# A decoder block in one kernel: three product-key units prepared beside the attention to the context, and three expert tiles put in a conditional block

## The chip, the core and the metric

The kernel runs on one core of one Trainium2 chip. The time is the device time of one execution in microseconds (us), from the first to the last instruction of the program and the little that lies around it. TensorE is called PE, its weight load PEld, VectorE DVE, ScalarE ACT, GpSimd POOL, SyncE SP.

## What is computed

All numbers are 32-bit floats. `x` has 16 sequences of 256 tokens with 256 features, `ctx` has 16 contexts of 120 rows. Cut to what matters:

```python
x = x + self_attention(layernorm(x))               # 16 heads, rotary, causal
x = x + attention_to(ctx)(layernorm(x))            # 16 heads, biases
x = x + product_keys(layernorm(x))                 # below
x = x + band_attention(layernorm(x))               # 16 heads, +0.1 near the diagonal
x = x + context_flow(layernorm(x), ctx)            # bi-directional attention flow
x = x + experts(layernorm(x))                      # below

def product_keys(x):                               # per token, 8 heads
    q1, q2 = halves(x @ Wq + bq)                   # 2 x 32 per head
    v1, i1 = top_k(q1 @ K1.T, 10)                  # 64 keys each
    v2, i2 = top_k(q2 @ K2.T, 10)
    vals, best = top_k(v1[:, None] + v2[None, :], 10)
    h = gelu(x @ W_down[chosen].T) * softmax(vals)
    return h @ W_up[chosen]

def experts(x):                                    # 8 experts, 2 per token
    w = softmax(x @ Wr + br), kept for the two largest, normalised
    return sum(w[e] * (relu(x @ W1[e] + b1[e]) @ W2[e] + b2[e]) for e in two)
```

## The kernel before, in words

All of `x` stays in SBUF as 16 tiles `xt[b]` of 128 partitions x 2 x 256, one for a sequence (a *batch* here). The work comes in five stages, one behind the other; each opens its own pools of SBUF and PSUM, so that its first tiles and its first loads wait until the stage before has let go of the memory.

**Both first attentions** are one pipeline (`run`, L149). It goes through 32 sequences of work (16 batches of the self-attention, then 16 of the attention to the context), six stages deep: `prepare`, `ready`, `maxima`, `weigh`, `values`, `finish`. In a round `v` the stage `i` works on batch `v - i`. `maxima` and `weigh` are the *joint* stages: their score matmuls (L246) are woven pair by pair, and behind each pair DVE takes the row maxima (L274) and ACT the exponentials (L315). The others are generators; `others_go(k)` moves them on by `k` steps, in turn, between two pairs (`gap` of them), and what is left goes at the end of the round. The order on PE is that order, by hand (`manual_schedule`). On the other engines a scheduler orders the instructions. `fresh` (L113) makes the layernorm statistics for four batches at a time (L119, L120, L122, L123), `normalized` (L103) writes `xn`, `transposed` (L126) gives `xnT`. Both tags have two buffers here. The score tiles `sa` and `sb` have one PSUM buffer each. Every tile of the small projections shares the PSUM tag `t1` with two buffers.

**The product keys** (L533 to L811) work on 32 *units* of 128 tokens. Four parts follow each other, one round of the loop apart: `front` (L557: normalise, transpose, project with `wq`, L137, and multiply by the keys, L581), `lists` (L585: the 16 best of 64 keys for 8 heads x 2 halves, all on DVE, in 8 steps), `choice` (L608: the best sums, on DVE, POOL and ACT, ending in `slots`), `places` and `spread` (L707, L725: one-hot tiles on DVE, L714, and POOL, L721, multiplied on PE, L733, into a `gate`), and `dense` (L744: all 4096 hidden values, L137, gelu, gate, and the second product, L758). In round `v`, `front` is at unit `v+1`, `lists` at `v`, `choice` at `v-1`, `spread` at `v-2`, `dense` at `v-3`. The loop starts at `v = -1`, so `dense` has nothing to do in its first four rounds. PE and DVE follow the written order. Ahead of the loop `layernorm_stats` (L95) makes the statistics of all 32 units (L98 to L102) and `shift` (L767). The stage loads `wq`, `keys12`, `w_dn` (2 x 2 MB) and `w_up` (4 MB) on SP when its pool opens (L538 to L543). The zeroing of the buffer `rows` (L763) is written in this stage too, but it needs nothing, and the scheduler starts it at the head of the kernel.

**The band attention** is the same pipeline with other parts. **The context flow** sends every batch through about a dozen steps, and ends with the routing: for each token its two experts and, by a running count, its place among the tokens of each; POOL scatters the rows to `rows` in HBM (L1132).

**The experts** (L1224) run over `NTL = 2*4096/256 + 8 - 1 = 39` tiles of 256 rows. Each expert gets `ceil(count/256)` tiles, which is at most 39 in all, but may be fewer. On DVE a chain of small instructions (L1165 to L1221) works out which expert a tile has (`et`, `eti`) and which rows (`source`); tiles behind the last needed one take the last expert, and their results go to spare rows of the output. For each tile SP reads the expert's number into a register and loads its weights (L1227, 2 MB), POOL gathers the rows (L1235), PE transposes (L1242), multiplies (h, L137; y, L1273), ACT does the relu (L1269), DVE the share (L1281) and POOL adds the result to the output in HBM (L1282).

One more piece: the small vectors that are added to rows lie in `rowv` (779 numbers, loaded once, L80); `folded` (L398) uses three of its slices as a matmul's moving rows.

Of the kernel before, what the change touches and what calls it, by code (L numbers as in the profile page):

```python
# [11 lines left out]
F32 = mybir.dt.float32  # L12
# [6 lines left out]
P = 128  # L19
# [32 lines left out]
def tile_decoder(ctx: ExitStack, tc: tile.TileContext, a: dict, out: bass.AP, last: int = 6):  # L52
# [26 lines left out]
    rowv = T(cst, [1, N_ROWV], "rowv")  # L79
    nc.scalar.dma_start(rowv, a["rowv"])  # L80
# [10 lines left out]
    def row(c, n):  # L91
        return rowv[:, c : c + n]


    def layernorm_stats(wk):  # L95
        for i in range(NT):
            st = T(wk, [P, 6], "bnst")
            nc.vector.bn_stats(st, xt[i // 2][:, i % 2, :])  # L98
            nc.vector.bn_aggr(mv[:, i, :], st)
        std = T(wk, [P, NT], "std")  # L100
        nc.scalar.activation(std, mv[:, :, 1], AF.Sqrt, bias=eps)
        nc.vector.reciprocal(rstd, std)  # L102

    def normalized(wk, b):
        xn = T(wk, [P, 2, D], "xn")
        for t in range(2):
            i = 2 * b + t
            nc.vector.tensor_scalar(
                xn[:, t, :], xt[b][:, t, :], mv[:, i, 0:1], rstd[:, i : i + 1], ALU.subtract, ALU.mult
            )  # L110
        return xn

    def fresh(wk, b, group=4):  # L113
# [10 lines left out]
        return normalized(wk, b)  # L124
# [24 lines left out]
    def run(stages, n, gap, joint=(2, 3)):  # L149
# [5 lines left out]
        with tc.manual_schedule(engines={mybir.EngineType.PE}):  # L155
            for v in range(n + len(stages) - 1):
                going = {i: stage(v - i) for i, stage in enumerate(stages) if 0 <= v - i < n}
                pairs = [going.pop(i) for i in joint if i in going]
                others = deque(going.values())

# [26 lines left out]
    class Attention:  # L187
# [6 lines left out]
        def __init__(self, pools, prepare, ready, kts, causal=None, band=None, qbias=None, w=None, badd=None):  # L194
            self.wk, self.ps, self.psa, self.psb = pools
            self.prepare_, self.ready_, self.kts, self.causal, self.band = prepare, ready, kts, causal, band
            self.qbias, self.w, self.badd = qbias, w, badd
# [173 lines left out]
        def finish(self, b):  # L371
# [11 lines left out]
            for t in range(2):  # L383
# [3 lines left out]
                yield  # L387
            del self.c[b]
# [10 lines left out]
    def folded(st_pool, ps, w, bv, bo):  # L399
# [6 lines left out]
        nc.tensor.matmul(pb, lhsT=ones, rhs=row(bo, D), start=False, stop=True)  # L406
# [8 lines left out]
    rows = T(pool(ctx, "dr", 1, bass.MemoryType.DRAM), [NE * CAP, RW], "rows")  # L415

# [3 lines left out]
    with ExitStack() as st:  # L420
# [23 lines left out]
        def self_prepare(b, c):  # L444
            xnT = T(wk, [P, 2, S], "xnT")
            transposed(ps, fresh(wk, b), xnT)
# [39 lines left out]
        def cross_prepare(b, c):  # L486
            cT = T(wk, [P, 2, NQ], "cT")
            nc.sync.dma_start(cT, a["ctxT"][b].rearrange("(c p) q -> p c q", p=P))
            xnT = T(wk, [P, 2, S], "xnT")
            transposed(ps, fresh(wk, b), xnT)  # L490
# [9 lines left out]
        def cross_ready(b, c):  # L500
# [5 lines left out]
            for g in range(HG):  # L506
# [6 lines left out]

        wxo = wx[:, :, 4 * D : 5 * D]
# [4 lines left out]
                badd=folded(w1, ps, wxo, C_XBV, R_XBO),  # L519
# [8 lines left out]
        run([both(i) for i in range(6)], 2 * B, lambda v: 2 if v - 2 < B else 3)  # L528
# [4 lines left out]
    with ExitStack() as st:  # L533
# [3 lines left out]
        wq = T(w3, [P, 2, PH * PK], "wq")  # L537
        nc.sync.dma_start(wq, a["p_wq"].rearrange("(c p) e -> p c e", p=P))  # L538
        keys12 = T(w3, [P, 2 * P], "keys12")
        nc.sync.dma_start(keys12, a["p_keys"])  # L540
# [16 lines left out]
        def front(u, res):  # L557

            b, t = divmod(u, 2)
            xn = T(wk, [P, D], "xn")  # L560
            nc.scalar.activation(
                xn, xt[b][:, t, :], AF.Identity, bias=shift[:, u : u + 1], scale=rstd[:, u : u + 1]
            )
            pt = T(ps, [P, 2, P], "t1")
            for dc in range(2):
                nc.tensor.transpose(pt[:, dc, :], xn[:, dc * P : (dc + 1) * P], ident)
            xnT = res["xnT"] = T(wk, [P, 2, P], "xnT", bufs=5)
            nc.scalar.copy(xnT, pt)
            yield
            pq = T(psb, [P, 4, P], "big")  # L570
            for c in range(4):
                project(pq[:, c, :], wq, c * P, P, xnT)
            qT = T(wk, [P, 4, P], "qT")
            for c in range(4):
                nc.scalar.activation(qT[:, c, :], pq[:, c, :], AF.Identity, bias=col(C_PBQ + c))
            yield
            sc = res["sc"] = T(wk, [P, 2 * PH, PK], "sc", bufs=2)
# [831 lines left out]
```

## Time and profile before

| | us |
|---|---|
| median of three runs | 3760.42 (3752.77 to 3763.39) |
| the profiled execution, its own time | 3756.87 |
| its span, first to last instruction | 3754.9 |
| PE busy | 3418.5 (91%) |
| DVE busy | 2275.5 (61%) |
| POOL busy | 1629.4 (43%) |
| ACT busy | 1605.9 (43%) |
| mean granted PE clock | 0.954 |

The stages lie so on the span: the two attentions end at about 758, the product keys at about 2319, the experts' matmuls run from 3177 to the end. A busy PE is not PE at its peak: its matmuls are pipelined and their ends are modelled. The view by windows gives the busy time of each engine in a stretch, and the clock that the throttle granted to PE there; the timeline gives single instructions with their start and length; the view by lines gives groups with the mean duration and the idle time ahead of them; the chain is what ended last, followed back from the end.

### The profile page before, as it was taken

The numbers are of one execution on the slowest core, as the hardware profiler recorded it, in microseconds if no ns is written. First come the engines' busy times: TensorE is split into PE (matmuls) and PEld (weight loads), VectorE is DVE, ScalarE is ACT, GpSimd is POOL, SyncE is SP. The second block draws the span as 40 slices with busy tenths as digits, with TensorE's granted clock in tenths as the row PEclk, the third lists the DMA queues.
The fourth block names the chain that finished last, engine by engine and source line by source line (L and its number), as shares of the span: only waits on it lengthen the run. The fifth ranks groups of instructions, "written<-read, shape, count | busy, mean of one in ns | idle before, by whom it ended". The sixth has DMA issues, their size and how long they took to land. (4 is left out here: it accounts for less than half of the span.)

```text
span 3754.9 us, 131060 instructions
## 1 busy us (share of the span) xinstructions
PE 3418.5 (91%) x57482; PEld 2837.3 (76%) x57482; DVE 2275.5 (61%) x9235; ACT 1605.9 (43%) x2831; POOL 1629.4 (43%) x1614
## 2 busy tenths in 40 slices
PE   6999999948999999999999998799988997999998
PEld 3666677737888888888888887576665885888887
DVE  6777633389888888888888873344443554111111
ACT  2455566524444444444444433355553552323322
POOL 2323200016666666666666664244443233333332
PEclk8999999959999999999999999799997987999999
DMA  9300000020000000000000000000001113655554
GB/s 327 113 2 2 4 8 10 3 97 4 4 4 4 4 4 4 4 4 4 4 4 4 4 4 17 1 2 1 2 1 44 43 52 113 187 176 183 185 173 134
DMA packets 49326, 182.00 MB, mean 48 GB/s; under 512 B 14889, under 2 KB 36785, under 8 KB 42354
## 3 DMA queue, kind: packets, MB, share of 16 engines
q1 hardware_dynamic: 29840, 144.22, 11.0%
q0 software_dynamic: 18048, 29.14, 3.7%
q8 instruction: 451, 7.39, 0.8%
q14 instruction: 121, 0.99, 0.1%
q10 hardware_dynamic: 866, 0.26, 0.0%
HBM read 150.66 MB, written 57.15 MB: 55 GB/s over the span
## 5 line engine op out<-in xcount | busy, mean ns | idle before, releaser
L721 POOL TENSOR_TENSOR hot<-hot,w 104x1024 f32<-104x1024 f32 x256 | 523.0, 2043 | 291.7 <-DVE hot L714 180.8
L714 DVE TENSOR_TENSOR hot<-wij,iota 104x1024 f32<-104x1024 f32 x512 | 598.9, 1212 | 55.7 <-ACT w L704 46.8
L137 PE MATMUL hid<-xnT,w_dn 128*128 128x128 f32 x4096 | 525.5, 281 | 4.4 <-issue 4.3
L137 PEld LDWEIGHTS hid<-xnT,w_dn 128*128 128x128 f32 x4096 | 484.7, 193 | 16.1 <-issue 6.4
L274 DVE TENSOR_REDUCE q<-sa 128x4 f32<-128x1024 f32 (+1 forms) x192 | 231.2, 1204 | 428.9 <-PE sb L246 248.5
L758 PE MATMUL acc<-w_up,hg 128*128 128x256 f32 x2048 | 482.6, 381 | 0.0
L752 POOL TENSOR_TENSOR hg<-hg,gate 128x512 f32<-128x512 f32 x256 | 342.2, 1337 | 242.0 <-ACT hg L751 242.0
L246 PE MATMUL sa<-kT,qT 32*128 32x256 f32 (+2 forms) x3072 | 350.9, 355 | 90.3 <-DVE q L274 60.9
L733 PEld LDWEIGHTS t<-hot,hot 104*32 104x32 f32 x32768 | 308.8, 110 | 156.0 <-POOL hot L721 111.3
L733 PE MATMUL t<-hot,hot 104*32 104x32 f32 x32768 | 338.7, 199 | 89.0 <-POOL hot L721 84.9
L315 ACT ACTIVATE pT<-sb 128x1024 f32<-128x1024 f32 (+1 forms) x288 | 294.8, 1023 | 276.2 <-PE sb L246 237.6
L758 PEld LDWEIGHTS acc<-w_up,hg 128*128 128x128 f32 x2048 | 372.5, 191 | 42.7
L740 ACT COPY gate<-t 128x512 f32<-128x512 f32 x256 | 270.8, 1058 | 244.9 <-PE t L733 244.9
L246 PEld LDWEIGHTS sa<-kT,qT 32*128 32x128 f32 x3072 | 240.9, 192 | 172.3 <-DVE q L274 93.7
L246 PE MATMUL sb<-qmT,kT 32*128 32x256 f32 (+2 forms) x2560 | 344.4, 390 | 7.7 <-ACT pT L315 7.2
L326 POOL TENSOR_TENSOR pT<-pT,bandf 128x260 f32<-128x260 f32 x256 | 183.9, 739 | 248.8 <-ACT pT L315 248.8
L137 PE MATMUL h<-xT,wt 128*128 128x256 f32 x1248 | 279.7, 382 | 6.0 <-ACT xT L1264 6.0
L751 ACT ACTIVATE hg<-hid 128x512 f32<-128x512 f32 x256 | 153.6, 600 | 304.1 <-PE hid L137 303.6
L1273 PE MATMUL y<-wt,hT 128*128 128x256 f32 x1248 | 276.0, 379 | 0.6 <-DVE ys L1281 0.6
L1282 POOL DMA_INDIRECT out_y<-ys,toi x78 | 123.3, 1580 | 340.3 <-DVE ys L1281 306.0
L137 PEld LDWEIGHTS h<-xT,wt 128*128 128x128 f32 x1248 | 224.1, 190 | 55.2 <-ACT xT L1264 10.5
L1273 PEld LDWEIGHTS y<-wt,hT 128*128 128x128 f32 x1248 | 237.0, 190 | 33.2 <-DVE ys L1281 1.0
(289 smaller groups left out, 5824.8 us busy)
## 6 DMA issues: line engine op xcount, KB each, us to landing
wt<-in_m_w SPq DMA_DIRECT2D x39, 2052.0 KB, 8.6
rows<-in_zeros SPq DMA_DIRECT2D x32, 1040.0 KB, 28.7
x<-in_x SPq DMA_DIRECT2D x16, 256.0 KB, 4.3
w_dn<-in_p_dn SPq DMA_DIRECT2D x2, 2048.0 KB
w_up<-in_p_up SPq DMA_DIRECT2D x1, 4096.0 KB, 23.6
out_y<-x SPq DMA_DIRECT2D x16, 256.0 KB, 2.5
cT<-in_ctxT SPq DMA_DIRECT2D x32, 120.0 KB, 2.0
cx<-in_ctx SPq DMA_DIRECT2D x16, 120.0 KB, 2.7
```

The costliest lines, as they stand in the source:

```text
L137: nc.tensor.matmul(o, lhsT=w[:, dc, c0 : c0 + n], rhs=rhs[:, dc, :], start=dc == 0, stop=stop and dc == 1)
L246: nc.tensor.matmul(sc[0 : ls.stop - ls.start, r, g, 0 : rs.stop - rs.start], lhsT=lhs[rows_, g0 + g, ls], rhs=rhs[rows_, g0 + g, rs], star ...
L274: nc.vector.tensor_reduce(to, sc[:, :, :, 0:nk], AX.X, ALU.max)
L315: nc.scalar.activation(pT[0:kn], sc[0:kn], AF.Exp, scale=1.0 / math.sqrt(DH))
L326: nc.gpsimd.tensor_tensor(own, own, self.bandf[:, kt, 0:n].unsqueeze(1).to_broadcast([P, ng, n]), ALU.mult,)
L714: nc.vector.tensor_tensor(t, wij[:, k, cs].unsqueeze(2).to_broadcast([HS, NC, PK]), iota[0:HS].unsqueeze(1).to_broadcast([HS, NC, PK]), AL ...
L721: nc.gpsimd.tensor_tensor(hot[1], hot[1], w[:, cs].unsqueeze(2).to_broadcast([HS, NC, PK]), ALU.mult)
L733: nc.tensor.matmul(pg[q * NLO : (q + 1) * NLO, t, :], lhsT=hi[:, t, i0 : i0 + NLO], rhs=hj[:, t, j0 : j0 + NLO], start=True, stop=True,)
L740: nc.scalar.copy(gate[:, :, c * NC : (c + 1) * NC].rearrange("p l t -> p t l"), pg)
L752: nc.gpsimd.tensor_tensor(hg, hg, gate[:, s * L : (s + 1) * L, :], ALU.mult)
L758: nc.tensor.matmul(acc, lhsT=hg[:, i, :], rhs=w_up[:, l, :], start=l == 0, stop=l == NLO - 1)
L1273: nc.tensor.matmul(y, lhsT=hT[:, fc, h * P : (h + 1) * P], rhs=w2[:, fc, :], start=fc == 0, stop=fc == FF // P - 1,)
```

## The change

Six edits. (An edit that only moves code, `front` and `lists`, is left out of the diff.)

1. **Early units.** `wq`, `keys12`, the `shift` tile, the lists of three units (`found`) and their `xnT` move to a pool that is open from the start until the product keys end; `wq` and `keys12` are loaded on ACT's queue ahead of everything in the first stage. `front` and `lists` become functions of the whole kernel. A seventh generator, `first_units`, runs in `run` beside the six stages from round 16 + 7 + 2 = 25 on, at up to four steps a round: it scales and sends units 0, 1 and 2 through `front` and `lists`. It uses the PSUM tag `t1`, the SBUF tag `ra` for `qT`, and the idle tiles `ks` of the self-attention for `sc`.
2. **Statistics per batch.** Behind each batch's `finish` in the attention to the context, `moments` makes that batch's mean and variance. The 32-unit statistics ahead of the product keys go; what stays there is one square root, one reciprocal and one `shift` for units 3 to 31.
3. **The loop** starts at `v = 1`, with `lists` and `front` from unit 3 on.
4. **Room.** `xn` and `xnT` in the first two attentions have one buffer in place of two.
5. **Rows.** `rowv` keeps its last 11 numbers. The three slices of 256 are loaded by `long_row` on ACT's queue where they are used.
6. **Conditional block.** `filled`, the number of tiles needed (the last of `ends`), is copied to an integer and read into a register of every engine. The first 36 tiles run as before; the last three (`OPEN = 3`) are in a block that is entered only if `filled > 36`.

```diff
-    rowv = T(cst, [1, N_ROWV], "rowv")
-    nc.scalar.dma_start(rowv, a["rowv"])
+    rowv = T(cst, [1, N_ROWV - R_BR], "rowv")
+    nc.scalar.dma_start(rowv, a["rowv"][:, R_BR:N_ROWV])
...
+    def long_row(pool_, c):
+        t = T(pool_, [1, D], "long_row")
+        nc.scalar.dma_start(t, a["rowv"][:, c : c + D])
+        return t
...
-    def run(stages, n, gap, joint=(2, 3)):
+    def run(stages, n, gap, joint=(2, 3), side=None):
...
                 others = deque(going.values())
+                if side is not None and v >= side[0]:
+                    others.append(islice(side[2], side[1]))
...
+            if self.then is not None:
+                self.then(b)
             del self.c[b]
...
-        nc.tensor.matmul(pb, lhsT=ones, rhs=row(bo, D), start=False, stop=True)
+        nc.tensor.matmul(pb, lhsT=ones, rhs=long_row(st_pool, bo), start=False, stop=True)
...
+    EARLY = 3
+    w0 = pool(early, "w0")
+    wq = T(w0, [P, 2, PH * PK], "wq")
+    nc.scalar.dma_start(wq, a["p_wq"].rearrange("(c p) e -> p c e", p=P))
+    keys12 = T(w0, [P, 2 * P], "keys12")
+    nc.scalar.dma_start(keys12, a["p_keys"])
+    shift = T(w0, [P, NT], "shift")
...
+    def scaling(us):
+        nc.scalar.activation(rstd[:, us], mv[:, us, 1], AF.Sqrt, bias=eps)
+        nc.vector.reciprocal(rstd[:, us], rstd[:, us])
+        nc.vector.scalar_tensor_tensor(shift[:, us], mv[:, us, 0], -1.0, rstd[:, us], ALU.mult, ALU.mult)
...
-            xnT = T(wk, [P, 2, S], "xnT")
-            transposed(ps, fresh(wk, b), xnT)
+            xnT = T(wk, [P, 2, S], "xnT", bufs=1)
+            transposed(ps, fresh(wk, b, bufs=1), xnT)
...
+        def moments(b):
+            for t in range(2):
+                st_ = T(wk, [P, 6], "bnst")
+                nc.vector.bn_stats(st_, xt[b][:, t, :])
+                nc.vector.bn_aggr(mv[:, 2 * b + t, :], st_)
+
+        def first_units():
+            yield
+            for b in range((EARLY + 1) // 2):
+                scaling(slice(2 * b, min(2 * b + 2, EARLY)))
+            yield
+            for u in range(EARLY):
+                units[u]["sc"] = ks[u % 2].rearrange("p t h r -> p (t h r)").rearrange("p (g k) -> p g k", k=PK)
+                yield from front(u, units[u], wk, ps, lambda *shape: (ps, [P, *shape], "t1"), ("ra", F32, 1))
+                for _ in lists(units[u], wk):
+                    yield
...
-        run([both(i) for i in range(6)], 2 * B, lambda v: 2 if v - 2 < B else 3)
+        run([both(i) for i in range(6)], 2 * B, lambda v: 2 if v - 2 < B else 3, side=(B + 7 + (EARLY + 1) // 2, 4, first_units()))
...
-        layernorm_stats(wk)
-        shift = T(w3, [P, NT], "shift")
-        nc.vector.scalar_tensor_tensor(shift, mv[:, :, 0], -1.0, rstd, ALU.mult, ALU.mult)
+        scaling(slice(EARLY, NT))
...
-            for v in range(-1, NT + 3):
+            for v in range(EARLY - 2, NT + 3):
...
-                listing = lists(units[v]) if 0 <= v < NT else iter(())
+                listing = lists(units[v], wk) if EARLY <= v < NT else iter(())
-                fronting = front(v + 1, units[v + 1]) if v + 1 < NT else iter(())
+                fronting = front(v + 1, units[v + 1], wk, ps, big) if EARLY <= v + 1 < NT else iter(())
...
+        endi = T(w6, [P, 1], "endi", U32)
+        nc.vector.tensor_copy(endi, ends[:, NE - 1 : NE])
+        filled = nc.values_load(endi[0:1, 0:1], min_val=1, max_val=NTL)
...
-        for j in range(NTL):
+        def experts_tile(j):
...
+        OPEN = (NE - 1) // 2
+        for j in range(NTL - OPEN):
+            experts_tile(j)
+        with tc.If(filled > NTL - OPEN):
+            for j in range(NTL - OPEN, NTL):
+                experts_tile(j)
```

## The prediction

> **What bounds the kernel now.** I read the view by windows first, since the mean share of an engine says nothing of a single stage. Columns: stretch, length, busy time (and count) of PE, PEld, DVE, ACT, POOL, then the granted PE clock, DMA share, GB/s.
>
> ```profile
> 556.00:738.00 182.00, 172.73 (x2326) 139.77 (x2320) 69.00 (x118) 114.42 (x226) 8.70 (x13) 1.00 0.03 7
> 758.00:804.40 46.40, 15.91 (x58) 12.44 (x59) 33.84 (x195) 9.24 (x21) 0.19 (x1) 0.60 0.48 195
> 804.40:824.60 20.20, 7.87 (x25) 5.34 (x23) 19.14 (x172) 5.12 (x13) 3.36 (x9) 0.50 0.00 1
> 824.60:866.50 41.90, 22.54 (x1054) 19.47 (x1054) 41.72 (x207) 11.75 (x21) 19.81 (x17) 0.62 0.01 3
> 866.50:913.60 47.10, 45.36 (x1250) 41.23 (x1247) 42.32 (x219) 22.63 (x35) 31.45 (x26) 0.97 0.02 4
> 3702.20:3743.20 41.00, 39.98 (x190) 33.87 (x189) 4.14 (x16) 13.02 (x27) 9.30 (x6) 1.00 0.44 122
> ```
>
> In the attention to the context (row 1) PE is the bound: 172.7 of 182 us. From 758 to 866.5 (rows 2 to 4) PE is idle for more than half of the time and DVE sets the pace: this is the fill of the product-key pipeline. From 866.5 both are full. At the end (row 6) PE is full again. The timeline says what the fill consists of:
>
> ```profile
> 779.81 0.18 DVE L99 BATCH_NORM_AGGREGATE mv<-bnst 128x2 f32<-128x6 f32 x1
> 780.14 1.28 ACT L101 ACT_TABLE_LOAD   x1 [23.61 <-DVE mv L99]
> ...
> 790.87 0.35 DVE L594 MAX8 v<-sc 128x8 f32<-128x64 f32 x2 [8.51 <-ACT sc L582]
> ...
> 804.40 0.58 DVE L628 TENSOR_TENSOR sums<-v 128x160 f32<-128x160 f32 x2
> ...
> 821.94 0.88 PE L702 MATMUL wij<-ident,slots 128*104 128x128 f32 x3 [8.37 <-POOL slots L692]
> ...
> 866.47 3.46 PE L137 MATMUL hid<-xnT,w_dn 128*128 128x128 f32 x16
> ```
>
> Statistics until 780, `front` of unit 0 until 790.87, its `lists` until 804.40 (13.5 us, eight steps of 1.69), its `choice` beside `lists` of unit 1 until the one-hot tiles begin at 824.6, the spreading of unit 0 beside `lists` of unit 2, and the first dense matmul at 866.5. The chain of what ended last (start, length, what) shows the end:
>
> ```profile
> 3698.53 3.72 PE y L1273 x16
> ...
> 3739.70 3.47 PE y L1273 x16
> ...
> 3743.95 3.85 DMA out_y<-ys,toi
> ...
> 3749.62 1.77 POOLq L1405
> ```
>
> The 36th tile's last matmul ends at 3702.2, the 39th's at 3743.2; what comes behind takes 11.7.
>
> **The fill.** (a) From 758.0 to 804.4, 46.4 us go. In their place stay the last batch's two pairs of statistics behind its last addition at 757.8 (0.43 and 0.18 us each, L98 and L99: some 1.6 with the 0.41 addition), a table load of 1.28, a root of 0.32, a reciprocal of 0.35 and a shift of 0.19: 3.9. Saved 42.5. (b) `choice` of unit 0 up to the one-hot tiles took 20.2, with 11.8 us of list steps among it on DVE (seven of 1.69). Without them it is a chain: sums and the first maxima to the first POOL instruction 2.8, POOL 0.8, table load and exponential 1.8, products 2.0, POOL 2.5, den and a last POOL product 1.1, transposes and copy 1.2: 12.2, so I take 12.5. Saved 7.7. (c) From 824.6 to 866.5 DVE was busy for 41.7 of 41.9 us; `lists` of unit 2 is 13.5 of these. POOL's 19.8 do not take over. I give 1 us back to a one-hot tile that waits. Saved 12.5. Together 62.7, with the first dense matmul some 46 us behind the end of the attention. `w_dn` and `w_up` (8.4 MB) are no obstacle: at the 329 GB/s that DMA reached in the first 60 us, they need 25.5 us. Bounds: 50 (all of (c) and (b) back to latency but 7.5) and 66 (no second square-root wait).
>
> **What the three units cost where they go.** Shares of the view by lines (busy us, mean ns, idle before):
>
> ```profile
> L581 PE MATMUL big<-keys,qT 128*128 128x256 f32 x256 | 70.9, 402 | 6.1 <-ACT qT L575 4.0 <-ACT sc L582 2.0
> L137 PE MATMUL big<-xnT,wq 128*128 128x128 f32 x512 | 69.5, 294 | 1.5 <-ACT xnT L568 1.5
> L566 PE MATMUL t<-ident,xn 128*128 128x128 f32 x64 | 13.3, 293 | 25.3 <-ACT xn L561 25.3
> ```
>
> For 32 units 153.7, so 4.8 each and 14.4 for three: PE is the bound there, so all of it counts. DVE takes 3 x 13.5 = 40.6 us of lists and 16 x 1.2 of statistics, of which the stretch has room for 113 (182 - 69); ACT some 3.6 a unit (0.6, 0.37, 4 x 0.37, 2 x 0.58) and two table loads, into 68 idle. But order matters: `sa` has one buffer, so each pair of score matmuls waits for the maxima of the pair before:
>
> ```profile
> PE sa L246 <- DVE q L274: 6.8, 11, 1.3
> ```
>
> That is the wait of PE in 556:738. A list step of 1.69 us that DVE takes up behind one maximum (1.16 us) delays the next by at most what the two exceed the pair's own distance: in the tightest pairs (about 2.2 us) 0.65. With 38 steps that is 25 us at the worst; at best PE's 9.3 idle us swallow as much of the matmuls. I take +5, nearest to the 6.8 of that row. Sum +19.4.
>
> **Small things.** `wq` and `keys12` (0.64 MB) now run ahead at the start, where DMA is full (344 GB/s until 22 us) and the first matmul, at 21.5, waits for `wx`, the last of 6.5 MB: 0.655 MB at 0.329 MB a us = +2.0 (bounds 0 and 4, if the two queues share badly). On ACT's queue their two issues (0.4 us each) stand ahead of `rope` and `causal`, first needed at 31.9; on SP's the loads of `w_dn` go out 0.9 us earlier. In the old place they were hidden beside the statistics. One buffer for `xn` and `xnT`: the next batch's normalisation needs only that the transposes of the round before are done, 18.15 us earlier (the distance of two rounds): 0. `long_row`: a load (1 KB) beside a larger one, `wx`, `wa` or `wl`; in the last place I take +1, bounds 0 and 2. The moved statistics (19.5 us) and the lists fall into the 113 idle us of DVE; without that cover they would cost what they save.
>
> **The conditional block.** The routing of the reference's own inputs gives the experts 1079, 603, 1315, 729, 1422, 993, 898 and 1153 rows: 5+3+6+3+6+4+4+5 = 36 tiles. 36 is not above 36, so the block isn't entered, and 3743.2 - 3702.2 = 41.0 us go. The 11.7 us at the end stay. Added: DVE reads `filled` in the middle of the chain that POOL's first gather waits for. The trace shows no read on DVE; on SP, from the number ready (3160.0) to the first weight load issued (3162.18), it was at most 2.2. I take +2, bounds 0 (put behind the chain) and 2.2. PE, ACT, POOL and SP read it while they wait for `source` anyway. At the block every engine compares and jumps; the trace shows no jump. It can't be below 0, and the nearest long row is that last stretch of 11.7, in which the program winds up; I take +2, nearest to the 2.0 of the smallest regular load (`cT`), and 10 as the upper end. Queued behind the jump is only the program's end.
>
> The program's own text is streamed too: the page's table has "q8 instruction: 451, 7.39", 16 KB a packet. The Trainium skill speaks against the jump here ("Runtime: NRT & Kernel Launch", Instruction fetch mechanics): a jump whose target isn't in the loaded window makes the sequencer fetch that page by DMA first. It gives no price; with one load as above it would be the +2 that I have, by the compare-and-branch of about 108 ns ("Advanced Engine Details and Errata", Control Flow Timing) the sum would be 2 us lower. No row here tells which.
>
> **Sum.** -62.7 + 14.4 + 5 + 2 + 1 - 41 + 2 + 2 = -77.3. The profiled execution took 3756.9, so 3679.6; the median shown is 3.5 above it, so I say 3681.
>
> **Rivals.** (1) *The block is entered* (a 37th tile): then 41 stay, and the pipeline starts again behind a block that isn't woven with the one before, as at 3165.7 to 3177.6, 12 us from gather to first product: 3756.9 - 62.7 + 14.4 + 5 + 2 + 1 + 4 + 12 = 3733. For it: only that I counted outside the chip; the nearest expert is 31 rows from a boundary. 4%. (2) *The side work jams the attention*: list steps stand ahead of maxima in nearly every pair, or POOL, ACT and the two `t1` buffers hold the transposes up; 38 steps at a whole 1.69 are 64 in place of 5: 3739. Against it: DVE is busy for 69 of 182. 7%. (3) *Slower*: with one `xn` and one `xnT`, the chain of two normalisations (0.81), transposes (0.6) and copy (0.59) with its signals, some 2.4 us, stands on PE's path in each of 32 rounds: +77, which eats the gain; if the value projections of the round before (2 us) have to be read off first too, 4.4 x 32 = 141, and the time is 3821. It decides from 2.4 us a round. Against it: the trace has the last `xn` written at 649.9 and its transposes at 666.5, so there are 16 us of lead to lose before anything waits. 3% slower, 3% near nothing. (4) *More than forecast*: PE swallows the added matmuls and neither read nor jump costs: 3756.9 - 66 - 41 + 14.4 - 9 = 3655. 4% beyond.
>
> **Numbers.** My forecast with its bounds has 79%. Low: as (4), 3655. High: 3756.9 - 50 - 41 + 14.4 + 25 + 4 + 2 + 2.2 + 10 = 3723. A measurement of this kernel can tell about 0.3% (11 us) from no change. Faster, that is under 3749: the forecast, (1), (2) and (4), 94%; same 3%; slower 3%.
>
> **What would show it.** Right: in the window view, the stretch between the attention's last addition and the first dense matmul is about 46 us, not 108; no L98 row; a round in the attention that holds side steps is about 20 us, not 18.15; PE's last product comes behind 36 tiles; first matmul at 23.5. Wrong: PE waits on `DVE q L274` well above 12 us; `POOL hot` waits in the first spreading round; 39 weight loads; more than 5 us between POOL's last add and the end beyond the 11.7 of before.

## The result, and the profile after

The changed kernel takes 3712.65 us (median of 4 runs, 3711.95 to 3720.23) against 3759.36 for the kernel before (4 runs, 3752.77 to 3763.39): a ratio of 0.9882, 95% interval 0.9863 to 0.9901. The forecast was 3681, in a range of 3655 to 3723. The direction and the range held; the gain is 46.7 us where 77 to 79 were forecast. The two profiled executions have spans of 3754.9 and 3710.2, 44.7 apart, and can be cut at the same landmarks:

| stretch (us) | before | after | measured | forecast |
|---|---|---|---|---|
| start to the first product | 21.5 | 25.4 | +3.9 | +2 |
| to the end of the first batch in the attention to the context | 497.8 | 490.4 | -7.4 | 0 |
| from there to the last batch's end | 238.9 | 297.1 | **+58.2** | +19.4 |
| to the first dense product (the fill) | 108.3 | 49.3 | -59.0 | -62.7 |
| to the start of the last dense products | 1445.2 | 1446.6 | +1.4 | 0 |
| to `source` (last attention, router) | 852.9 | 850.2 | -2.8 | +1 |
| to the first expert product | 13.0 | 13.3 | +0.3 | +2 |
| to the last expert product's end | 569.0 | 523.5 | -45.4 | -41 |
| to the end | 8.3 | 14.4 | +6.1 | +2 |

The landmark of the fifth row is the start of the last run of 16 products of L137 in the product keys. A batch ends with its second addition to `x` (L386; in the kernel after L384). The end of the first batch in the attention to the context is the landmark that the expectations below call the 18th addition or round 18. The first six rows are the three units' part: -5.7 in place of -40.3. The last three are the block's: -39.0 in place of -37.

In the window view (stretch, length, busy time and count of PE, PEld, DVE, ACT, POOL, then granted clock, DMA share, GB/s), the kernel before, cut at these landmarks:

```profile
519.30:758.20 238.90, 224.94 (x2936) 179.41 (x2936) 87.37 (x155) 145.22 (x283) 11.75 (x18) 0.99 0.03 6
758.20:866.50 108.30, 46.32 (x1135) 37.25 (x1135) 94.50 (x572) 26.12 (x55) 23.18 (x27) 0.59 0.21 85
```

and the kernel after:

```profile
515.80:812.90 297.10, 254.40 (x3014) 200.40 (x3014) 156.18 (x639) 165.22 (x320) 13.00 (x19) 0.94 0.02 5
812.90:862.20 49.30, 22.80 (x1057) 19.48 (x1057) 37.44 (x143) 15.71 (x31) 23.28 (x28) 0.63 0.42 173
862.20:908.40 46.20, 46.17 (x1248) 42.09 (x1248) 39.15 (x204) 22.54 (x34) 31.49 (x26) 0.95 0.02 4
```

The fill is halved, as foreseen. The attention in the first row is what failed: PE's busy time grows by 29.5 us for 78 matmuls more, the clock falls from 0.99 to 0.94, and PE's idle time rises from 14.0 to 42.7. The view of waits of PE (engine, line, what it waited for: us in total, times, longest) in 515.8 to 809 says on what:

```profile
PE sa L244 <- DVE q L272: 21.8, 20, 3.6
PE t L127 <- DVE xn L104: 9.9, 2, 5.1
```

The first was the row `6.8, 11, 1.3` of before in 556 to 738 (8.1 in 13 waits over the whole 519.3 to 758.2); the second did not exist. The prediction named the first as a sign that it is wrong, "well above 12 us". How such a wait comes about stands in the timeline of VectorE (start, us, what). Each step of `lists` begins with a pair of L473:

```profile
609.81 0.35 DVE L473 MAX8 v<-k 128x8 f32<-128x64 f32 x2 [4.40 <-ACT k L462]
...
611.52 0.33 DVE L473 MAX8 v<-k 128x8 f32<-128x64 f32 x2
...
613.20 0.34 DVE L473 MAX8 v<-k 128x8 f32<-128x64 f32 x2
...
614.90 0.33 DVE L473 MAX8 v<-k 128x8 f32<-128x64 f32 x2
...
616.58 1.14 DVE L272 TENSOR_REDUCE q<-sa 128x8 f32<-128x960 f32 x1
```

and in that of TensorE at the same place:

```profile
612.44 0.40 PE L244 MATMUL sa<-kT,qT 32*128 32x120 f32 x4
...
613.61 1.03 PE L461 MATMUL t<-keys,ra 128*128 128x256 f32 x4
617.78 0.42 PE L244 MATMUL sa<-kT,qT 32*128 32x120 f32 x1 [3.14 <-DVE q L272]
```

The scores were ready at 612.8. Their maximum came at 616.6, because four list steps, 6.8 us, stood ahead of it in VectorE's order. The written order, TensorE's, hands out a round's side steps one at a time, in turn with the steps of the other stages; VectorE's order is the scheduler's, and it put four list steps in a row. The clock behind that stop, in the window view (the clock is the third number from the end; the last section shows it behind the stop of 2.38 us that ends at 627.38):

```profile
616.00:617.70 1.70, 0.00 (x0) 0.00 (x0) 1.70 (x9) 0.00 (x0) 0.00 (x0) 1.00 0.00 0
617.70:619.00 1.30, 1.22 (x18) 1.23 (x22) 1.30 (x14) 0.00 (x0) 0.00 (x0) 0.60 0.06 13
619.00:620.00 1.00, 1.00 (x14) 0.78 (x8) 1.00 (x12) 0.23 (x1) 0.00 (x0) 0.50 0.00 0
620.00:621.00 1.00, 1.00 (x6) 0.91 (x5) 1.00 (x11) 0.98 (x2) 0.00 (x0) 0.50 0.00 0
621.00:622.00 1.00, 1.00 (x4) 0.53 (x2) 1.00 (x6) 0.66 (x2) 0.00 (x0) 0.81 0.04 8
```

So a stop is paid twice: once as idle time, and once as a time at half clock behind it, 3.4 us here (about 618.0 to 621.4). In the stretch from 515.8 to 812.9 the clock was at half six times, each behind a stop of 2.4 to 5.1 us: twice for 3.4 us, three times for 6.8, once for 10.2, 37.5 us in all. In the kernel before, from 519.3 to 758.2, there was one such time of 3.4.

### The profile page after: what moved, and what is told of

It reads as the page before. It is cut to its first block, busy times and chain, and to the rows that moved or that the text cites. A ratio compares the mean times of both kernels' runs of the same rounds, so it can differ in the third digit from the quotient of the medians.

```text
span 3710.2 us, 130592 instructions
## 1 busy us (share of the span) xinstructions
PE 3376.6 (91%) x57278; PEld 2801.8 (76%) x57278; DVE 2267.3 (61%) x9204; ACT 1601.4 (43%) x2812; POOL 1615.5 (44%) x1602
## 5 line engine op out<-in xcount | busy, mean ns | idle before, releaser
L757 POOL TENSOR_TENSOR hot<-hot,w 104x1024 f32<-104x1024 f32 x256 | 523.5, 2045 | 276.1 <-DVE hot L750 188.7
L133 PE MATMUL h<-xT,wt 128*128 128x256 f32 x1152 | 258.0, 382 | 5.0 <-ACT xT L1301 5.0
L1310 PE MATMUL y<-wt,hT 128*128 128x256 f32 x1152 | 254.5, 379 | 0.0
L1319 POOL DMA_INDIRECT out_y<-ys,toi x72 | 113.6, 1578 | 310.7 <-DVE ys L1318 286.1
L133 PEld LDWEIGHTS h<-xT,wt 128*128 128x128 f32 x1152 | 206.8, 190 | 50.2 <-ACT xT L1301 9.0
L1306 ACT ACTIVATE hT<-h,wt 128x256 f32<-128x256 f32 x288 | 136.6, 474 | 243.5 <-PE h L133 231.0
```

The lines of the kernel that those rows point to most:

```text
L133: nc.tensor.matmul(o, lhsT=w[:, dc, c0 : c0 + n], rhs=rhs[:, dc, :], start=dc == 0, stop=stop and dc == 1)
L757: nc.gpsimd.tensor_tensor(hot[1], hot[1], w[:, cs].unsqueeze(2).to_broadcast([HS, NC, PK]), ALU.mult)
L1310: nc.tensor.matmul(y, lhsT=hT[:, fc, h * P : (h + 1) * P], rhs=w2[:, fc, :], start=fc == 0, stop=fc == FF // P - 1,)
```

## The experiments

My theory after the result was that list steps standing ahead of row maxima (and late normalised rows) make nearly all of the excess in the attention; the rivals were the added products themselves, the single `xn` and `xnT` buffers, and the block. All kernels are read by the same landmarks; each ratio is to executions of the kernel before in that run's own session, whose medians lay between 3753.2 and 3759.4. "Attention" is the stretch from the end of the first batch in the attention to the context to the end of its last, "fill" from there to the first dense product.

| kernel | us, median | ratio to before (95%) | attention | fill |
|---|---|---|---|---|
| before (profiled span 3754.9) | 3759.36 | 1 | 238.9 | 108.3 |
| after | 3712.65 | 0.9882 (0.9863 to 0.9901) | 297.1 | 49.3 |
| block alone | 3712.85 | 0.9885 (0.9869 to 0.9902) | 239.0 | 108.2 |
| 36 tiles, no block | 3714.31 | 0.9897 (0.9873 to 0.9922) | 297.4 | 49.3 |
| fronts only, 2 units | 3700.26 | 0.9852 (0.9836 to 0.9868) | 247.6 | 80.6 |
| own statistics name | 3705.53 | 0.9862 (0.9846 to 0.9879) | 283.5 | 49.8 |
| two scopes, VectorE by hand | 3717.96 | 0.9891 (0.9875 to 0.9908) | 302.1 | 50.3 |
| scope per round | 3666.15 | 0.9762 (0.9746 to 0.9779) | 291.6 | 49.3 |
| scope per round, VectorE by hand | 3646.17 | 0.9700 (0.9682 to 0.9718) | 279.5 | 48.9 |
| before, scope per round | 3698.92 | 0.9849 (0.9833 to 0.9866) | 237.2 | 107.4 |
| four things together | 3653.77 | 0.9732 (0.9714 to 0.9751) | 270.7 | 48.0 |
| the same, thinner | 3652.41 | 0.9731 (0.9712 to 0.9750) | 263.7 | 48.8 |
| the same, own name too | 3627.33 | 0.9666 (0.9653 to 0.9679) | 263.2 | 49.5 |
| load order alone (one execution) | 3713.45 | | 297.4 | 48.8 |

### The block alone

Before, with only this:

```
+        endi = T(w6, [P, 1], "endi", U32)
+        nc.vector.tensor_copy(endi, ends[:, NE - 1 : NE])
+        filled = nc.values_load(endi[0:1, 0:1], min_val=1, max_val=NTL)
...
+        for j in range(NTL - OPEN):
+            experts_tile(j)
+        with tc.If(filled > NTL - OPEN):
+            for j in range(NTL - OPEN, NTL):
+                experts_tile(j)
```

> The kernel before with the conditional block alone (the read of the number of tiles, 36 tiles, the block of three behind them); attention and product keys are as before. My theory now, from the trace after: three tiles go (45 us) and 7.4 us are added between the last scatter and the end, so the span is 3754.9 - 38 = 3717. The prediction's own terms (-41, +2 for the read, +2 for the jump) give 3718: the same sum from other parts, told apart by the time from the last scatter issued to the end, 12.5 us by the theory, 7 by the prediction. Rival: the number read on five engines takes time on the chain ahead of the first gather: then the first product of the experts comes 2 us or more later than before (3177.6).

Measured: 3712.85, span 3711.5. The first product of the experts stands at 3173.3, 13.0 behind `source` as before, so the read costs nothing on that chain and the rival falls. The trace says why: only SP reads the number there (at 3154.5). ACT, PE, DVE and POOL read it behind their instructions for the last tile, directly ahead of the jump (at 3690.4, 3693.4, 3697.4 and 3699.0). From the last scatter's issue (3698.9) to the end are 12.6 us, as the theory said. What follows is larger than the question: the block alone gives **the whole of the change's gain**. 3712.85 and 3712.65 can't be told apart, so the three units' part, forecast at -40.3, came to some 3 us by the medians (46.7 less 43.5, each against its own before) and to 5.7 by the landmarks above; these times can't tell that from nothing.

### 36 tiles without the block

After, with `for j in range(NTL - OPEN): experts_tile(j)` and neither `filled` nor the block.

> The kernel after with 36 tiles and neither the read nor the block; it leaves out the last three tiles, which these inputs don't fill. Theory: the block costs 7.4 us at the end (the jump, the software queue's catching up, a longer drain), so the span is 3710.2 - 7.4 = 3703, with 5 us from the last scatter issued to the end. Rival: the 12.5 us there are the last scatters' own landing, whatever the block: 3710, no change.

Measured: 3714.31, the median of ten executions, of which eight lie between 3709.38 and 3716.40, one at 3753.59 and one at 11697.1; what held up these two is not known. The median lies within the spread of the kernel after, and no gain shows. In its profile the last product ends at 3704.2 and the span at 3714.7, 10.5 us; in the kernel after it is 14.4, in the kernel before 8.3. From the last scatter's issue to the end it is 8.6, against 12.5 and 5.1. So the block's own price at the end is 3.9 us, not 7.4: the theory had half of it. The other 2.2 of the +6.1 stay without the block; why is open. That rests on one profile of 36 tiles without a block; all eleven profiles with the block have 13.9 to 14.7 behind the last product, the two with 39 tiles 8.3 and 8.5. In the times the 3.9 don't show; the profiled execution of this run is 8.4 us longer elsewhere.

### The fronts without the lists

After, with two early units and the lists of both made behind the attention (and a tile name of its own for the new statistics, as in the next run):

```
-    EARLY = 3
+    EARLY = 2
...
-                for _ in lists(units[u], wk):
-                    yield
...
         with tc.manual_schedule(engines={mybir.EngineType.PE, mybir.EngineType.DVE}):
+            for u in range(EARLY):
+                for _ in lists(units[u], wk):
+                    pass
             for v in range(EARLY - 2, NT + 3):
```

> The kernel after with two early units instead of three, with a tile name of its own for the new statistics, and with the lists of these two units made behind the attention; beside the attention are only their products with the keys (4.8 us of TensorE each) and the statistics. The fill is some 27 us longer for that. Theory (the lists' place on VectorE is what costs): the stretch from the 18th addition to the last, 239 us before and 283.5 with the statistics' own name, is 239 + 9.6 = 249, at most 253, and TensorE's waits for the maxima are back at 7. Rival (the added products, their two shared buffers in PSUM, or ScalarE's copies and table loads hold the attention up): 265 or more.

Measured: attention 247.6, where 249 was expected of the theory and 265 of the rival. Its rows of the window view and of the waits of PE:

```profile
522.20:769.80 247.60, 231.94 (x2988) 185.14 (x2988) 107.72 (x219) 154.28 (x303) 12.83 (x18) 1.00 0.03 6
```

```profile
PE sa L244 <- DVE q L272: 6.7, 11, 1.3
```

The wait is back at the 7 us of before, and the clock at 1.00. The products of a unit cost (247.6 - 238.9) / 2 = 4.35 us, near the 4.8 of the prediction. The lists, then, are what costs. With a fill that is 31 us longer the kernel is still 12 us faster than the change. Against the next run, which has the statistics' own name and all lists beside the attention, it is 5 faster, but the two spreads overlap (3696.42 to 3705.68 and 3701.48 to 3707.93) and this one has a unit less: in that order, lists beside the attention cost about what they save in the fill.

### A name of their own for the statistics

```
-                st_ = T(wk, [P, 6], "bnst")
+                st_ = T(wk, [P, 6], "bnm")
```

> The kernel after, with a tile name of their own (two small buffers) for the new statistics per batch, which in the change share the two buffers of the statistics that the next group's normalisation needs. Theory (the group's statistics queue behind the new ones for a buffer and so start only when the round's last addition is done, which makes the normalised rows late): the waits of TensorE for them, 5.1 and 4.8 us, go, with the half clock behind them another 6 to 8: span 3692 to 3700. Rival (the single buffer of the normalised rows makes them late): both waits stay, 3710 within 3.

Measured: attention 283.5, 13.6 less, as expected. No wait for `xn` is left in it (waits of PE, 515.8 to 809):

```profile
PE sa L244 <- DVE q L272: 24.6, 22, 3.6
PE t L359 <- ACT oS L353: 4.0, 8, 0.8
```

`xn` and `xnT` still have one buffer each in this kernel, so the rival falls: the late normalised rows came from `bnst`. The buffers of a name are handed out in program order, so the statistics of a group of four batches (`fresh`) had to wait behind the new statistics of the round before, which wait for that round's last addition. Then eight pairs of statistics, a root and two normalisations stand between that addition and TensorE's transposes. The time fell by only 7.1, since the rounds ahead of the stretch are longer again: the first batch ends 9.5 us later than in the kernel after (525.3 to 515.8).

### VectorE's order by hand

Three runs belong together. In the first, the attention's one scope of hand-written order is cut in two, at the first round with side steps, and VectorE is ordered by hand in the second:

```
-        with tc.manual_schedule(engines={mybir.EngineType.PE}):
-            for v in range(n + len(stages) - 1):
+        two = (0, n + len(stages) - 1) if side is None else (0, side[0], n + len(stages) - 1)
+        for first, end in zip(two, two[1:]):
+          with tc.manual_schedule(engines={mybir.EngineType.PE} | ({mybir.EngineType.DVE} if first else set())):
+            for v in range(first, end):
```

> The kernel after with two scopes in the attention to the context: up to round 24 TensorE alone is ordered by hand, from round 25 (the first with side steps) VectorE too. The first and the last attention are as in the kernel after. Theory (list steps ahead of maxima and the half clock behind each stop): the waits of TensorE for the maxima fall from 22.4 us to under 8, the stretch from the 18th addition to the last falls from 297 to some 275 to 283, and the time by 14 to 22, to 3690 to 3698. If the order of VectorE has no part in it and only the scopes have: 3710, with the stretch at 297.

The second, the earliest of the three to run, has one scope for each round, in all three attentions, and VectorE by hand from the same round on:

```
+        for v in range(n + len(stages) - 1):
+            by_hand = {mybir.EngineType.PE}
+            if side is not None and v >= side[0]:
+                by_hand.add(mybir.EngineType.DVE)
+            with tc.manual_schedule(engines=by_hand):
```

> The kernel after, with VectorE's order in the rounds that hold side steps written by hand as TensorE's is, so that no more than one or two list steps stand between two row maxima. Theory (four list steps ahead of a maximum hold TensorE 2 to 5 us at a time, and each such stop leaves its clock at half for some 8 us): the wait of TensorE for the maxima falls from 20.1 us to 8 or less, the attention ends 12 to 25 us earlier, span 3685 to 3698. It cannot reach the waits for the normalised rows (5.1 and 4.8 us), and the eight statistics of a group now stand in line ahead of maxima, so one new stop of 6 us may come. Rival 1 (single buffers of the normalised rows, or the added matmuls themselves): 3710, within 4. Rival 2 (order by hand makes VectorE wait for what ScalarE hands it): slower than 3710.

The third is the second without the two lines that add VectorE:

> The kernel after, with one scope of the hand-written order for each round of an attention instead of one scope for the whole attention; TensorE alone is ordered by hand, VectorE is left to the scheduler. It separates the two things that the run with VectorE by hand changed (that run took 62 us less than the kernel after: some 36 of it in the last attention, which has no side work, some 12 in the first, and 18 in the stretch with side work, from 297 to 279.5 us between the 18th round's addition and the last). If the scopes alone are worth the first two, this run takes some 48 us less than the kernel after (3662), and its stretch with side work stays near 297. If VectorE's order is what counts everywhere, it takes 3710.

Measured: 3717.96, 3646.17 and 3666.15. In the first the wait for the maxima is gone, and another has taken its place (waits of PE, 520 to 823):

```profile
PE t L127 <- DVE xn L104: 24.8, 7, 8.0
PE sa L246 <- DVE q L274: 6.0, 14, 0.9
```

In an order by hand the normalisation stands where it is written, behind the round's list steps and directly ahead of the transposes that need it; left to the scheduler it runs up to a round ahead (in the own-name run, written by 549.7 and transposed from 565.8 on). So **my theory was right about what the wait is and wrong about the cure**: the attention became 5 us longer, not 14 to 22 shorter.

The second run gained three times what I expected of it, and the third says from what: 46.5 us come from the scopes (36.8 of them in the stretch with the last attention, which has no side work; the attention with side steps stays at 291.6). With a scope per round, VectorE by hand is then worth 20.0 more, 12.1 of it in the attention; the waits for the maxima are 8.2 there and two waits for `xn` are left (5.1 and 7.1).

### What a scope per round does without the change

The edit of the third run, on the kernel before.

> The kernel before, with one scope of the hand-written order for each round instead of one for each attention: what that does without the change. If the scopes are worth 48 us by themselves and have nothing to do with the side work, this takes 3757 - 48 = 3709; if their worth comes from the change (shared buffers, late statistics), it takes 3757.

Measured: 3698.92, 57 us less than before, without any part of the change. The scopes are a gain by themselves. What they do is seen in the last attention: TensorE's waits in 2330 to 2900, first of before, then of this kernel:

```profile
PE sa L246 <- DVE q L274: 50.5, 62, 1.3
```

```profile
PE sa L246 <- DVE q L274: 17.9, 31, 1.3
```

A batch there takes 26.9 us in place of 28.3 (additions from 2463 to 2705, nine apart, and from 2464 to 2747, ten apart). At the seams of the scopes the compiled order mixes the last score products of a round with the first transposes and products of the next (L131 and L137, behind the scores at 2570.9 and 2573.4), and TensorE doesn't wait there; with one scope, three pairs of scores have only the 0.66 us of the transposes of L361 between them, and TensorE waits 0.74 and 0.75 us (until 2608.6 and 2611.1). That this mixing is all of the 49 us in that stretch was not shown.

By the same comparison the three units' part does not pay on this ground either: the scopes alone give 3698.92, and with the whole change 3666.15, 32.8 less, where the block alone was worth 43.5 on the kernel before.

### The load order

```
         nc.sync.dma_start(wx, a["l0x_w"].rearrange("(c p) e -> p c e", p=P))
+        nc.sync.dma_start(wq, a["p_wq"].rearrange("(c p) e -> p c e", p=P))
+        nc.sync.dma_start(keys12, a["p_keys"])
```

> The kernel after with the query weights and keys of the product keys loaded on the queue behind the weights of the attention to the context, as the only edit. Theory (0.66 MB ahead of those weights delay the first product, 25.4 us in place of 21.5): first product at 21.5 to 22.0 and a span some 4 us shorter, 3706. Rival (the first product waits for the input's batches or the short rows on the other queue): 25, no change.

Measured, one run: first product at 22.98, 2.4 us earlier, span 3711.7. Half of the expected 4 at the start, and none of it at the end: the first batch ends at 519.7, 3.9 later than in the kernel after. A gain ahead of the first attention was lost within it; why is open. (The same code gave a first batch 2.6 us apart, counted from the first product, in the executions of the kernel before and of the block alone, so this is near what one execution can tell.)

### Together

One scope per round, VectorE by hand from the first side round, the load order, and the statistics for the attention to the context made per batch behind the additions of the attention before it (`then=moments` there too, and `fresh` with the root alone):

> The kernel after with four things together: one scope per round; VectorE by hand from the first round with side steps; the statistics that the attention to the context needs made per batch behind each last addition of the attention before it (so a group's normalisation has only its root left); and the query weights and keys of the product keys loaded behind the weights of the attention to the context. Theory: from the 3646 of the run with VectorE by hand go the two waits for the normalised rows (12.2 us, 5.1 and 7.1) with some 8 us of half clock behind them, and 4 us at the start: 3620 to 3630. Rival: with both engines in line, the waits move to another tile (the attention's outputs, the copies of ScalarE), and only the 4 us at the start are gained: 3638 to 3646.

Measured: 3653.77, worse than the 3646.17 that it was built on. The attention did fall, to 270.7, but the first batch ended 19.7 us later (523.1 to 503.4). TensorE's waits up to 500:

```profile
PE t L127 <- DVE xn L104: 10.2, 2, 5.1
```

That is the wait of the change, now in the first attention: I had given `moments` a second user and left it on `bnst`, so the first attention's own statistics queued behind it. My expectation missed what an earlier run had already shown.

> The run with four things together, with three side steps a round from round 23 on instead of four from round 25. Theory (what a round pays is the list steps that stand ahead of a maximum or a normalisation): fewer in a round delay less, though in more rounds, so the time is the same to 8 us shorter. Rival (each round that holds lists pays a fixed price, in half clock): 13 rounds in place of 9.5 pay, and the time is 5 to 10 us longer.

Three side steps a round from round 23 on. Measured: 3652.41, attention 263.7, 7 us shorter than with four steps; the times can't be told apart. The rival, a fixed price for each round with lists, has nothing for it.

> The thinner version of the four things together, with the statistics per batch in a tile name of their own. In that version the first attention's normalised rows wait again (two waits of 5.1 us in the trace, the same queueing for the two shared buffers, now in the first attention, whose 13th round's addition stands at 319.5 us against 311.5 with VectorE by hand alone, though its first product is 2.9 us earlier). Theory (a shared small buffer orders statistics that have nothing to do with each other): these waits and their half clock go, 8 to 13 us: 3637 to 3645 by the median of 3652 of that version. Rival (the first attention is late for another reason, the statistics' place itself): 3648 to 3656.

Measured: **3627.33** (5 runs, 3626.22 to 3631.86), 25 us less than the run before it, where 7 to 15 were expected: the first batch ends at 504.3 in place of 517.5, and the product keys and the last attention, whose code the edit leaves as it is, take 3.7 and 5.3 us less, so some 9 of the 25 are not explained. It beats both kernels, at 0.9666 of before (0.9653 to 0.9679) and about 0.977 of after (3627.33 / 3712.65). Its window row:

```profile
504.30:767.50 263.20, 240.41 (x3018) 189.53 (x3014) 143.56 (x605) 158.86 (x314) 12.99 (x19) 0.99 0.02 6
```

All three units are in it, lists too: the attention is 24.3 us longer than before, of which 13 are products, for a fill that is 58.8 shorter, and the clock is 0.99. Placed so, the three units' part comes nearer to the 40 us that the prediction gave it: some 28 us net, if the scopes alone with the block are taken as 3698.9 - 43.5 = 3655.4 (an estimate; that kernel wasn't run, and VectorE's order by hand, the load order and the statistics are among the 28).

## Why the prediction was right and where it was wrong

- **Right: the fill.** -59.0 for -62.7, and the sizes of the steps can be read off. (b) The first `sums` at 813.92 to the first one-hot tile at 826.40 are 12.5, as said. (a) saved 45.2, not 42.5: the last batch's root, 3.9 us that I left on the path, has nothing to do with units 0 to 2. (c) saved 6.1, not 12.5, where I had given 1 us back for a one-hot tile that waits. The sum, 59.0, is within the bounds of 50 and 66. What ate the rest of (c) is seen in TensorE's waits in the first spreading round, in the kernel before (824.6 to 866.5) and after (826 to 862.2):

```profile
PE t L733 <- POOL hot L721: 21.1, 7, 6.2
```

```profile
PE t L769 <- issue: 8.3, 6, 2.3
PE t L769 <- POOL hot L757: 5.3, 2, 4.8
```

  With the lists gone TensorE waits for POOL's tiles a quarter as long, but it stops six times in the middle of its products with nothing in the profile that it waits for ("issue"); before has no such stop there. Each of the six ends 1.3 to 1.5 us behind the landing of a packet of the program's text (the first: landed at 834.70, TensorE goes on at 836.12). That TensorE waited for its text is likely by that, but was not shown.
- **Right: the products,** 13.0 for 14.4 (three times 4.35). **Right: the block isn't entered;** 36 weight loads. The three tiles went with 45.4 us, not 41. The prediction misread the chain: 3743.2 is where the first 16 of the 39th tile's 32 second products end. Its last product ends at 3746.6, so the three tiles were 44.4 us (3702.2 to 3746.6) in the trace of before already, and what comes behind 8.3, not 11.7.
- **Right in kind, too low: the end.** +6.1 for +2, inside the bounds of 0 and 10; 3.9 of it is the block's. The last 13.5 us of the kernel after and of the block alone hold one packet of the program's text, those of before and of the 36 tiles without a block none. TensorE's compare-and-branch took 3.60 us, with a packet 1.0 us behind its start; those of the other engines took 0.05 to 0.06. But TensorE was through it at 3696.3, ahead of POOL's last scatter (3697.7), so it is not on the way to the end. Of the two pages of the Trainium skill that the prediction weighed, the one on instruction fetch ("Runtime: NRT & Kernel Launch", Instruction fetch mechanics) fits the packets; that the 3.9 us are such a fetch is not shown. The about 108 ns for a compare-and-branch ("Advanced Engine Details and Errata", Control Flow Timing) don't explain 3.9. The read cost nothing on its chain (0 of the bounds 0 to 2.2), since it isn't there: DVE reads behind the last tile, at 3696.2. The start cost 3.9 of at most 4.
- **Right, as far as the waits show: one buffer for `xn` and `xnT` costs 0.** With the statistics' own name no wait for `xn` is left in the attention to the context; two buffers were not run against it. Rival (3) had the wrong cause, but the wait that it named did come, from another shared buffer.
- **Wrong: "+5" for the waits in the attention.** It was 58.2 - 13.0 = 45.2. The step that failed: "A list step of 1.69 us that DVE takes up behind one maximum (1.16 us) delays the next by at most what the two exceed the pair's own distance". It takes one step between two maxima for granted. I had read that from the place of the steps in the written order, which holds for TensorE, and VectorE's order isn't written by hand. Four steps in a row are 6.8 us, and 31.6 of the 45.2 remain for the lists (283.5 - 238.9 - 13.0) when the statistics have their own name. Rival (2) had this mechanism, at 7% and 64 us, and I put it aside for VectorE's 69 busy us in 182: a share of busy time, where an order was asked for. Its price was miscounted too: of the 38 side steps only 24 are list steps (three units of eight; 3 x 13.5 is 40.6 us), so it should have said 40.6 us and 3715 in place of 64 and 3739, and the 25 us at the worst should have been 24 x 0.65 = 15.6.
- **Wrong: "The moved statistics (19.5 us) and the lists fall into the 113 idle us of DVE".** The statistics' time did; their buffers didn't. Sharing `bnst` cost 13.6 in the attention, by the run with a name of their own, where I had nothing.
- **Missing: the clock.** No term of the sum priced what a stop does to it. In the attention the mean granted clock went from 0.99 to 0.94. The 37.5 us at half clock withheld 18.8, against 1.7 before: 17.1, or some three tenths of the 58.2, as an estimate. It agrees with TensorE's busy time, which grew by 29.5 where the products account for 13.0.

The sum therefore missed by the attention, 38.8 us too low, against 7.4 that the rounds ahead of it gave (why is open) and smaller errors that nearly cancel. The range held because its upper end, 3723, carried 25 us for the waits and 10 for the block; with the 15.6 of the right count of steps it would have been 3714, some 1.5 us above the measured time. That it held is in good part luck.

## What to carry to other kernels

Work that is put beside a bound engine is hidden only if its place in the *other* engine's order is known: ask who writes that order, how many of the new steps can stand ahead of one instruction that the bound engine waits for, and multiply by that, not by one. A new user of a small shared buffer is a new order between things that have nothing to do with each other; give it a name of its own. And price each longer stop of TensorE with the slow clock that can follow it. Before a change is credited, run its parts alone: here one part had the whole gain, and an edit of the scopes without the change had more.

## What the runs showed of the hardware

- Short stops can be enough to halve the clock. After an idle time of 3.14 us it was 0.5 for some 3.4 us, and after one of 2.38 us (with a gap of 0.67 five us earlier) again:

```profile
627.00:628.00 1.00, 0.62 (x16) 0.62 (x20) 0.32 (x1) 0.00 (x0) 0.00 (x0) 1.00 0.00 0
628.00:629.00 1.00, 1.00 (x17) 0.79 (x12) 0.16 (x1) 0.25 (x1) 0.00 (x0) 0.60 0.00 0
629.00:630.00 1.00, 1.00 (x3) 0.82 (x3) 1.00 (x1) 0.77 (x1) 0.00 (x0) 0.50 0.00 0
630.00:631.00 1.00, 1.00 (x10) 0.33 (x13) 0.22 (x2) 0.00 (x0) 0.00 (x0) 0.50 0.00 0
631.00:632.00 1.00, 1.00 (x18) 0.49 (x10) 0.81 (x3) 0.18 (x1) 0.00 (x0) 0.69 0.00 0
```

  The Trainium skill ("TensorE: Matmul & The Clock Gate", HAM oscillation — how this bites in real kernels) gives the rule that idle gaps above about 3.4 us have to be avoided. The slow times here were 3.4, 6.8 or 10.2 us, one to three times 3.4; the two gaps above were shorter, so the rule as a threshold would have called both stops harmless. The length of a stop alone doesn't decide either: in the run with the statistics' own name no slow time followed the stops of 3.14 us (from 616.1) and 3.13 (from 684.0), and one did follow the stops of 2.28 behind each of them (slow from 624.4 and 692.7).
- At the end of a program with the block that is jumped over, POOL's queue shows, behind the last scatter, a semaphore step of 1.63 to 1.64 us and a drain of 5.99, in the kernel after, in the block alone and in the last version alike; without the block there is only a drain, begun beside the last scatter (8.06 us with 36 tiles, 4.42 in the kernel before).
